# Post-norm attention layer with a LoRA-mixture FFN on one core: the last two attention parts and the FFN as one sequence, W_base in four pieces, matmuls on a constant at the start, the last tile in halves

## The chip, the core and the metric

The kernel runs on one core of a Trainium2 chip. The metric is the device time of one execution in microseconds. A core has TensorE (PE: matmuls, with its weight loads PEld beside it), VectorE (DVE), ScalarE (ACT), GpSimd (POOL) and SyncE (SP). Here SP only issues transfers. Every engine works through its own instructions in program order, and waits where an operand or a free buffer is missing.

## The reference

`x` is 2 x 512 x 512 in fp32, the attention has 32 query heads and 8 key/value heads of 128, and the FFN is a 512 x 512 linear map plus a routed low-rank part of 4 active experts of rank 8.

```python
def attn(x):                       # causal, rotary, R = 4 query heads per key head
    q, k, v = x @ Wq + bq, x @ Wk + bk, x @ Wv + bv
    p = softmax(mask(rope(q) @ rope(k).T / sqrt(128)))
    return (p @ v) @ Wo + bo

def ffn(x):
    y = x @ W_base.T + b_base
    alpha = softmax(log(prior[active] + 1e-12) + (x @ router_W.T + router_b)[active])
    return y + sum_e alpha_e * 2 * (x @ A_e.T) @ B_e.T

x = layernorm(x + attn(x))
x = layernorm(x + ffn(x))
```

## The kernel before

The order of every instruction is written out by hand (a manual schedule). The work is cut into 16 units (a key head of one batch), each unit into 4 parts (128 query tokens, times 4 heads), and each part into 4 score steps of 32 tokens times 4 heads. One `slot(T)` issues, for step T, the scores of step T, the masked maximum and the exponentials of step T-1, the reciprocals of T-2, the normalisation of T-3, the 32x32 block transposes of T-4, and so on. Four steps make a part, which `blocks_out` writes to DRAM (`db`) and `blocks_in` reads back as a fully transposed tile (`pT`). `weigh` multiplies `pT` with the values (`pc`, line 535), `context_out` copies the result (`ctxT`), and either `wo_products` (a Strassen form, for the first 14 units) or `wo_mm` with `wo_out` (plain, for the last two) adds the output projection into the residual `x_sb`. Scores stand in a PSUM pool `sc` of two buffers: the scores of step s+2 wait until the exponentials of step s have read theirs.

The stages that the change touches:

- **The start** (lines 170 to 183 and 889 to 912). POOL builds an identity, a mask row `maskw` and zeros. PE transposes the first four token tiles (`transpose_token_tile`, line 265) as they arrive, then computes the keys (line 346) and the four query heads (`q_mm`, also line 346) of unit 0, with the values (`v_tile`, line 333, added to the bias by DVE in line 338) behind query heads 1 to 3. All the value tiles use the bank `wx`. Then come the transposes of token tiles 4 to 7, and then the slots.
- **The experts.** In the first slot `gather_experts` lets DVE compute indices (lines 225 to 245), and POOL then issues eight indirect transfers (line 248), the fourth of which is `pr_act`. Four slots later `prior_weights` uses it: DVE line 295, a logarithm on ACT (line 297), DVE lines 300 to 304, and in slot -2 one tiny matmul on PE (`pl`, line 307). DVE's index computation stands behind the values `v_3` in DVE's order, and the matmul `pl` stands in PE's order behind 7 query products of unit 1.
- **W_base.** At slot `T_PROJ` = 237 the projection memory is given up and `wb_sb` is loaded into it with one transfer of 1 MB (line 924), before slot 237 issues its `blocks_in`. Its four transposes (bank `k`, copied to `wbT` by ACT, line 266) stand in slots 242 to 245. In slot 246 ACT computes two square roots for the first normalisation, which needs another activation table: the load stands before them, and another before the next exponential.
- **The end.** `Ffn` objects `f0[0]`, `f0[1]` (two tiles each of batch 0), `fa` (two tiles of batch 1), `fb` and `fc` (one tile each) go through: statistics, root, `centre`, `transpose` (x1T), `route` (`zl`), `logits`, `alphas`, `base` (four matmuls `py`, line 710), `low_rank` (`tz`, `zT`), `finish` (line 714, with the residual added by DVE in line 717), second statistics, root, `store`. The slots run to E+12 = 268, and after them the rest is written as a list. The last tile `fc` gets its residual through PE (`residual`, line 722), its statistics from PSUM (`finish_in_bank`), one scaling of 128x512 and one output transfer.

Of the kernel before, what the change touches and what calls it, by code (L numbers as in the profile page):

```python
# [9 lines left out]
F32 = mybir.dt.float32  # L10
# [5 lines left out]
P = 128  # L16
H = 32
G = 8
R = H // G
# [10 lines left out]
def postln_layer_kernel(  # L30
# [69 lines left out]
    outf = out.flatten_outer_dims()  # L100
# [13 lines left out]
    x_sb = const.tile([P, NT, HID], F32, name="x_sb")  # L114
# [16 lines left out]
    xT = proj.tile([P, KC, B * S], F32, name="xT")  # L131
# [33 lines left out]
    def load_x(t, n):  # L165
        nc.sync.dma_start(
            out=x_sb[:, t : t + n, :], in_=xf[t * P : (t + n) * P, :].rearrange("(t p) n -> p t n", p=P))


    make_identity(nc, ident)  # L170
    nc.gpsimd.memset(maskw, 0.0)

    tri = setup.tile([P, QB, BLK], F32, name="tri")
    nc.gpsimd.memset(tri, 0.0)
# [1 line left out]
        out=tri, in_=tri, pattern=[[-BLK, QB], [-1, BLK]], compare_op=ALU.is_ge,  # L176
# [84 lines left out]
    def transpose_token_tile(dst, src, pool, tag, copy):  # L261

        tp = pool.tile([P, KC, P], F32, tag=tag, name="tp")
        for c in range(KC):
            nc.tensor.transpose(tp[:, c, :], src[:, ts(c, P)], ident)  # L265
        copy(dst, tp)  # L266
# [49 lines left out]
    sc = {}  # L316
# [19 lines left out]
    def v_out(gg, t):  # L336
        v_sb[gg, t] = work.tile([P, VN], F32, tag="v", name=f"v_{gg}_{t}", bufs=11)
        nc.vector.tensor_tensor(v_sb[gg, t], psq["v", gg, t], wvs[gg][1], ALU.add)  # L338
# [191 lines left out]
    def weigh(p, j):  # L530
        u, i = parts[p]
        g, b = unit(u)
        if j == 0:
            psc[p] = ps_ctx.tile([P, R, P], F32, tag="ctx", name="pc")
        nc.tensor.matmul(  # L535
            psc[p], lhsT=v_sb[g // VG, b * TPB + j][:, ts(g % VG, D)], rhs=pT[p][:, :, ts(j, P)],
            start=(j == 0), stop=(j == i))

    def context_out(p):
        ctxT[p] = work.tile([P, R, P], F32, tag="ctxT", name=f"ctxT_{p}", bufs=3)  # L540
        nc.scalar.copy(ctxT[p], psc[p])  # L541
# [59 lines left out]
    def wo_mm(p, r):  # L601

        u, i = parts[p]
        if r == 0:
            pwo[p] = ps_wo.tile([P, HID], F32, tag=("wx", "wy")[p % 2], name="po")
        nc.tensor.matmul(  # L606
            pwo[p], lhsT=ctxT[p][:, r, :], rhs=wos[set_of(u)][:, r, :], start=(r == 0), stop=(r == R - 1))

    def wo_out(p):
        u, i = parts[p]  # L610
        t = unit(u)[1] * TPB + i
        nc.vector.tensor_tensor(x_sb[:, t, :], pwo[p], x_sb[:, t, :], ALU.add)


    class Norm:
# [4 lines left out]
            self.rstd = pool.tile([P, n], F32, name=f"rstd_{name}")  # L620
            self.pool = pool

        def stats(self, i, src):
            st = self.pool.tile([P, 6], F32, tag="st", name="st", bufs=2)
            nc.vector.bn_stats(st, src)
            nc.vector.bn_aggr(self.mv[:, i, :], st)

        def root(self, lo, hi):
# [7 lines left out]
    class Ffn:  # L636
# [15 lines left out]
            self.norm1.apply(i, self.tiles[i])  # L652

        def transpose(self, i, pool, tag):
            self.xT[i] = self.pool.tile([P, KC, P], F32, tag=f"x1T{self.where[i] % TPB}", name=f"x1T_{self.where[i]}")
            transpose_token_tile(self.xT[i], self.tiles[i], pool, tag, nc.scalar.copy)

        def route(self, i):
# [54 lines left out]
        def finish(self, i):  # L713
            nc.tensor.matmul(self.py[i], lhsT=self.zT[:, i, :], rhs=bmT, start=False, stop=True)  # L714
            t = self.where[i]
            self.y[i] = self.pool.tile([P, O], F32, tag=f"y{t % TPB}", name=f"y_{t}")
            nc.vector.tensor_tensor(self.y[i], self.py[i], self.tiles[i], ALU.add)
            self.norm2.stats(i, self.y[i])

        def residual(self, i):  # L720

            nc.tensor.matmul(self.py[i], lhsT=ident, rhs=self.tiles[i], start=False, stop=False)

        def finish_in_bank(self, i):

            t = self.where[i]
            self.y[i] = self.pool.tile([P, O], F32, tag=f"y{t % TPB}", name=f"y_{t}")
            nc.tensor.matmul(self.py[i], lhsT=self.zT[:, i, :], rhs=bmT, start=False, stop=True)
            self.norm2.stats(i, self.py[i])

        def store(self, i, src=None):
            self.norm2.apply(i, self.y[i], src)
            nc.sync.dma_start(out=outf[ts(self.where[i], P), :], in_=self.y[i])


    NP = len(parts)
# [8 lines left out]
    def put(slot, f):  # L745
        extra.setdefault(slot, []).append(f)
# [3 lines left out]
    def v_tile(gg, t, pool, tag):  # L750
        for c in range(KC):
            v_mm(gg, t, c, pool, tag)
# [135 lines left out]

    spare = ((ps_wo, "wx"), (ps_wo, "wy"), (ps_ctx, "ctx"), (ps_sc, "sc"))
    q_banks = ((ps_q, "qx"), (ps_q, "qy"), (ps_q, "qx"), (ps_wo, "wy"))  # L890
    for t in range(TPB):
        transpose_token_tile(xT[:, :, ts(t, P)], x_sb[:, t, :], *spare[t], copies[t % 2])
    tb = ps_sc.tile([P, H + G], F32, tag="sc", name="tb")
# [7 lines left out]
    for r in range(R):  # L901
        for c in range(KC):
            q_mm(0, r, c, *q_banks[r])
        for part in range(3):
            q_rope(0, r, part)
        if r:
            v_tile(0, r - 1, ps_wo, "wx")
            v_out(0, r - 1)
    v_tile(0, R - 1, ps_wo, "wx")
    v_out(0, R - 1)  # L910
    for t in range(TPB, NT):
        transpose_token_tile(xT[:, :, ts(t, P)], x_sb[:, t, :], *spare[t % 2 + 2], nc.scalar.copy)

    T_SETUP = 20
    for T in range(T_BEGIN, T_SETUP):
# [2 lines left out]
    T_PROJ = T_END - 19  # L918
# [5 lines left out]
    nc.sync.dma_start(out=wb_sb, in_=W_base.rearrange("(c p) n -> p c n", p=P))  # L924
    wbT = ffn_pool.tile([P, KC, O], F32, name="wbT")


# [3 lines left out]
    QX, QY, SC = (ps_q, "qx"), (ps_q, "qy"), (ps_sc, "sc")  # L931
    f0 = [Ffn(f"0{n}", [2 * n, 2 * n + 1], ffn_pool, K_BANK) for n in range(2)]
# [16 lines left out]
    for n, f in enumerate(f0):  # L949
        at = A + 5 + n * 8  # L950
        for k in range(2):
            put(at, lambda f=f, k=k: f.route(k))
        put(at, f.logits)
        put(at + 1, f.alphas)
        for k in range(2):
# [3 lines left out]
        for k in range(2):  # L959
            put(at + 5, lambda f=f, k=k: f.finish(k))  # L960
        put(at + 6, lambda f=f: f.norm2.root(0, 2))
        for k in range(2):
            put(at + 6, lambda f=f, k=k: f.store(k))
    put(E + 8, lambda: fa.norm1.root(0, 2))
    for k in range(2):
        put((E + 2, E + 7)[k], lambda k=k: fa.norm1.stats(k, fa.tiles[k]))
        put(E + 8, lambda k=k: fa.centre(k))
        put(E + 10, lambda k=k: fa.transpose(k, *SC))
        put(E + 11, lambda k=k: fa.route(k))
    put(E + 11, fa.logits)  # L970
    put(E + 12, fa.alphas)
    put(E + 9, lambda: (fb.norm1.stats(0, fb.tiles[0]), fb.norm1.root(0, 1), fb.centre(0)))
    put(E + 11, lambda: fb.transpose(0, *QX))
    for T in range(T_PROJ, E + 13):
        slot(T)
    for c in range(KC):
        fa.base(0, c, *SC)
    fc.norm1.stats(0, fc.tiles[0])
    fc.norm1.root(0, 1)
    fc.centre(0)  # L980
    fb.route(0)
    fb.logits()
    fb.alphas()
    fa.low_rank()
    for c in range(KC):
        fa.base(1, c, *SC)
    fc.transpose(0, *QY)
    fb.low_rank()
    fa.finish(0)
    fa.finish(1)  # L990
    fc.route(0)
    fc.logits()
    fc.alphas()
    fa.norm2.root(0, 2)
    fa.store(0)
    fa.store(1)
    for c in range(KC):
        fb.base(0, c, *QX)
    fb.finish(0)
    fc.low_rank()  # L1000
    for c in range(KC):
        fc.base(0, c, *QY)
    fc.residual(0)
    fb.norm2.root(0, 1)
    fb.store(0)
    fc.finish_in_bank(0)
    fc.norm2.root(0, 1)
    fc.store(0, fc.py[0])


# [48 lines left out]
```

## Time and profile before

The median of three runs is 849.96 us (849.74 to 852.04). The profile is one further execution.

| what | value |
|---|---|
| runs | 849.96 us median, 849.74 to 852.04 |
| the profiled execution, its own time | 849.14 us |
| its span, first to last instruction | 847.3 us |
| granted TensorE clock, mean | 0.994 |
| HBM traffic | 71.73 MB read, 44.04 MB written, 137 GB/s over the span |
| ACT exponentials, line 494 | 256 instructions, 124.2 us busy, 485 ns mean |
| PE context products, line 535 | 320 instructions, 166.4 us busy, 603 ns mean |
| PE scores, line 479 | 512 instructions, 161.8 us busy, 398 ns mean |

An fp32 matmul appears as two instructions, an fp32 transpose as one. A row of the timeline starts with the start in us from the beginning of the span and the time the merged instructions took; in square brackets stands how long the engine had been idle before, and what released it. SPq is SP's queue of transfers. A matmul's duration contains its way through the array, so that back-to-back matmuls overlap in these rows: the distance of their starts is what each costs.

### The profile page before, as it was taken

What the parts mean: (1) busy time and instruction counts of PE and PEld (TensorE: products, weight loads), DVE (VectorE), ACT (ScalarE), POOL (GpSimd) and SP (SyncE); (2) the same over time, 40 slices, a digit from 0 to 9 for tenths busy, and PEclk for the clock granted to TensorE, in tenths of its full rate; (3) what the DMA queues carried; (4) which work ended last, traced back from release to release, by engine and by line L of the source; (5) the groups of instructions that cost most, each with busy time, mean ns of one, the idle gap of its engine ahead of it and who ended that gap; (6) DMA issues with size and microseconds to landing.
All of it is one profiled execution on the core that took longest, in us unless ns stands there. A gap on an engine that the chain in (4) does not pass through costs nothing.

```text
span 847.3 us, 10606 instructions
## 1 busy us (share of the span) xinstructions
PE 827.3 (98%) x3161; PEld 573.9 (68%) x3161; DVE 594.2 (70%) x1952; ACT 351.1 (41%) x990; POOL 277.4 (33%) x308
## 2 busy tenths in 40 slices
PE   8999999999999999999999999999999999799987
PEld 4567677777777767777777777777777776554443
DVE  4468977787767877786767877786767869654354
ACT  1225454444435343444344353434444444562331
POOL 5474334233332334133332234353433324200000
PEclk9999999999999999999999999999999999999999
DMA  9017536463654555362644455472735436564201
GB/s 297 25 44 205 158 82 193 106 179 113 156 154 102 166 160 165 88 197 64 178 133 119 156 155 162 105 220 76 194 103 149 150 105 189 170 207 112 87 26 50
DMA packets 84779, 116.47 MB, mean 137 GB/s; under 512 B 6517, under 2 KB 64477, under 8 KB 82674
## 3 DMA queue, kind: packets, MB, share of 16 engines
q1 hardware_dynamic: 84210, 115.63, 47.4%
q0 software_dynamic: 448, 0.14, 0.2%
q8 instruction: 25, 0.41, 0.2%
q14 instruction: 32, 0.26, 0.1%
q10 hardware_dynamic: 64, 0.02, 0.0%
HBM read 71.73 MB, written 44.04 MB: 137 GB/s over the span
## 4 chain that ended last, share of the span: by engine, by line
PE 93%; DVE 4%; DMA 1%; ACT 1%; issue 0%; DVEq 0%; ACTq 0%
PE pc L535 16%; PE sc L479 14%; PE qx L420 11%; PE wx L420 11%; PE pp L346 10%; PE qy L420 8%; PE wy L420 8%; PE pv L333 6%; PE po L606 3%; PE py L710 3%; PE tp L265 1%; PE zl L663 1%; DMA pT<-db 1%; PE py L714 1%; DVE t L359 0%
## 5 line engine op out<-in xcount | busy, mean ns | idle before, releaser
L494 ACT ACTIVATE p<-sc,nmax 128x288 f32<-128x288 f32 (+15 forms) x256 | 124.2, 485 | 263.9 <-DVE nmax L487 207.3
L487 DVE CUSTOM_DVE_ANT_0 sc<-sc,maskw 128x288 f32<-128x288 f32 (+15 forms) x256 | 114.1, 446 | 158.3 <-PE sc L479 155.4
L535 PE MATMUL pc<-pT,v 128*128 128x512 f32 x320 | 166.4, 603 | 4.0 <-DMA pT<-db 4.0
L479 PE MATMUL sc<-kT,qT 128*128 128x160 f32 (+15 forms) x512 | 161.8, 398 | 0.2 <-ACT p L494 0.2
L502 ACT ACTIVATE p<-p,den 128x288 f32<-128x288 f32 (+15 forms) x256 | 133.5, 521 | 1.2 <-DVE den L498 1.0
L367 POOL TENSOR_TENSOR qT<-q,t 128x512 f32<-128x512 f32 x56 | 71.1, 1269 | 189.0 <-DVE q L366 189.0
L479 PEld LDWEIGHTS sc<-kT,qT 128*128 128x128 f32 x512 | 96.9, 190 | 29.6 <-issue 15.6
L407 POOL TENSOR_TENSOR cs<-ctxT 128x256 f32<-128x256 f32 x28 | 26.8, 956 | 195.6 <-PE wy L420 109.2
L541 ACT COPY ctxT<-pc 128x512 f32<-128x512 f32 x64 | 37.4, 585 | 122.8 <-PE pc L535 122.6
L510 DVE STREAM_TRANSPOSE zt<-p 128x128 f32<-128x128 f32 (+2 forms) x192 | 81.5, 425 | 0.0
L535 PEld LDWEIGHTS pc<-pT,v 128*128 128x128 f32 x320 | 57.1, 191 | 23.8 <-issue 7.0
L346 PE MATMUL pp<-xT,wk 128*128 128x512 f32 x128 | 65.0, 593 | 0.5 <-ACT xT L266 0.5
L333 PE MATMUL pv<-wv,xT 128*128 128x256 f32 x256 | 64.1, 380 | 1.1 <-DVE v L338 1.1
L333 PEld LDWEIGHTS pv<-wv,xT 128*128 128x128 f32 x256 | 48.4, 190 | 15.2 <-issue 7.4
L420 PE MATMUL wx<-wo,ctxT 128*128 128x256 f32 x224 | 58.1, 382 | 0.3 <-DVE den L498 0.3
L420 PE MATMUL qx<-xs,wq 128*128 128x256 f32 x224 | 58.0, 381 | 0.0
L512 DVE STREAM_TRANSPOSE zt<-p 128x32 f32<-128x32 f32 (+3 forms) x256 | 57.3, 224 | 0.1
L420 PEld LDWEIGHTS qx<-xs,wq 128*128 128x128 f32 x224 | 41.4, 190 | 22.3 <-issue 16.0
L420 PEld LDWEIGHTS wx<-wo,ctxT 128*128 128x128 f32 x224 | 43.0, 192 | 14.0 <-issue 8.6
L494 ACT ACTIVATION_READ_ACCUMULATOR p<-sc,nmax 128x1 f32 x256 | 49.8, 194 | 0.0
L592 DVE TENSOR_TENSOR x_sb<-wx,x_sb 128x256 f32<-128x256 f32 x112 | 46.9, 419 | 0.0
L359 DVE SCALAR_TENSOR_TENSOR t<-q,bqkT,rope_sb 64x512 f32<-64x512 f32 x56 | 43.0, 768 | 1.3
(224 smaller groups left out, 1334.8 us busy)
## 6 DMA issues: line engine op xcount, KB each, us to landing
db<-zt SPq DMA_DIRECT2D x64, 256.0 KB, 4.3
pT<-db SPq DMA_DIRECT2D x16, 1024.0 KB, 4.8
db<-zt SPq DMA_DIRECT2D x64, 192.0 KB, 3.3
pT<-db SPq DMA_DIRECT2D x16, 768.0 KB, 4.6
wq<-in_L_attn_Wq_dram SPq DMA_DIRECT2D x20, 512.0 KB, 4.9
wo<-in_L_attn_Wo_dram SPq DMA_DIRECT2D x10, 1024.0 KB, 7.5
db<-zt SPq DMA_DIRECT2D x64, 128.0 KB, 2.4
pT<-db SPq DMA_DIRECT2D x16, 512.0 KB, 4.1
```

What stands on the lines that cost most here:

```text
L333: nc.tensor.matmul(psq["v", gg, t], lhsT=xT[:, c, ts(t, P)], rhs=wvs[gg][0][:, c, :], start=(c == 0), stop=(c == KC - 1))
L346: nc.tensor.matmul(psq[key], lhsT=wt[:, c, cols], rhs=xT[:, c, ts(b, S)], start=(c == 0), stop=(c == KC - 1))
L367: nc.gpsimd.tensor_tensor(dst, t1[:].rearrange("p (n s) -> p n s", s=BLK), t2[:].rearrange("p (n s) -> p n s", s=BLK), ALU.add)
L420: nc.tensor.matmul(ps, lhsT=wt[:, c, :], rhs=xt[:, c, :], start=start and c == 0, stop=c == CH - 1, skip_group_check=True)
L479: nc.tensor.matmul(sc[s][:, :w], lhsT=qT[u][:, i * QB + n].rearrange("p r s -> p (r s)"), rhs=kT[u][:].rearrange("p n s -> p (n s)")[:, :w ...
L487: nc.vector.tensor_tensor_reduce(sc[s][:, :w], sc[s][:, :w], maskw[:, S - w :], -SCALE, -MASKED, ALU.add, ALU.min, nmax[s])
L494: nc.scalar.activation(ptile[s][:, :w], sc[s][:, :w], AF.Exp, bias=nmax[s], scale=-1.0, accum_out=rden[s])
L502: nc.scalar.activation(ptile[s][:, :w], ptile[s][:, :w], AF.Copy, scale=rden[s])
L510: nc.vector.transpose(z[:, :, last - i : last, n, :].rearrange("p q j s -> p j q s"), ptile[s][:, : i * P])
L512: nc.vector.transpose(z[:, : n + 1, last, n, :], ptile[s][:, i * P : w])
L535: nc.tensor.matmul(psc[p], lhsT=v_sb[g // VG, b * TPB + j][:, ts(g % VG, D)], rhs=pT[p][:, :, ts(j, P)], start=(j == 0), stop=(j == i))
L592: nc.vector.tensor_tensor(into, pw[k, bank], into, ALU.add)
```

## The change

- `maskw` is zeroed by DVE, and not by POOL. After it, three matmuls of 128x256 on that constant stand in front of PE's first transposes; nothing reads what they write.
- In the opening list the transposes of token tiles 4 to 7 go behind query head 2; the values follow behind heads 1 and 3 and after the loop, and alternate between the banks `wx` and `ctx`.
- `W_base` is loaded in four transfers of 256 KB at the ends of slots 237, 238, 241 and 242, behind these slots' `blocks_in`. Its transposes move from slots 242, 243, 244, 245 to 241, 242, 245, 246.
- The slots end at E+6 = 262. What followed is one list together with the last two parts' `weigh` and `wo_mm`: the second tile of `f0[1]` gets its `base` between the last `weigh` and the transposes of `fa`; the `finish` and `store` of `f0[1]` go behind the routing of `fa` and `fb`; `fa`'s second-normalisation steps go behind those of `f0[1]`.
- The last tile is computed in two halves of 256 columns in two banks: four matmuls, the residual and the low-rank part for each. Two statistics, one aggregate, two scalings, two output transfers, on SP's and on ACT's queue.
- The buffers for x1T and y have names of their own instead of shared tags.

```diff
+    nc.vector.memset(maskw, 0.0)
     make_identity(nc, ident)
-    nc.gpsimd.memset(maskw, 0.0)
...
-        def residual(self, i):
-
-            nc.tensor.matmul(self.py[i], lhsT=ident, rhs=self.tiles[i], start=False, stop=False)
...
+        def half(self, i, n, pool, tag):
+
+            cols = ts(n, O // 2)
+            py = self.py[i, n] = pool.tile([P, O // 2], F32, tag=tag, name="ph")
+            for c in range(KC):
+                nc.tensor.matmul(py, lhsT=self.xT[i][:, c, :], rhs=wbT[:, c, cols], start=(c == 0), stop=False)
+            nc.tensor.matmul(py, lhsT=ident, rhs=self.tiles[i][:, cols], start=False, stop=False)
+            nc.tensor.matmul(py, lhsT=self.zT[:, i, :], rhs=bmT[:, cols], start=False, stop=True)
...
+        def store_halves(self, i):
             t = self.where[i]
...
+            y = self.pool.tile([P, O], F32, name=f"y_{t}")
+            for n, queue in enumerate((nc.sync, nc.scalar)):
+                cols = ts(n, O // 2)
+                self.norm2.apply(i, y[:, cols], self.py[i, n])
+                queue.dma_start(out=outf[ts(t, P), cols], in_=y[:, cols])
...
+    idle = ps_sc.tile([P, 2 * P], F32, tag="sc", name="idle")
+    for _ in range(3):
+        nc.tensor.matmul(idle, lhsT=maskw[:, :P], rhs=maskw[:, : 2 * P], start=True, stop=True)
...
-        if r:
-            v_tile(0, r - 1, ps_wo, "wx")
-            v_out(0, r - 1)
-    v_tile(0, R - 1, ps_wo, "wx")
-    v_out(0, R - 1)
-    for t in range(TPB, NT):
-        transpose_token_tile(xT[:, :, ts(t, P)], x_sb[:, t, :], *spare[t % 2 + 2], nc.scalar.copy)
+        if r == 2:
+            for t in range(TPB, NT):
+                transpose_token_tile(xT[:, :, ts(t, P)], x_sb[:, t, :], *spare[t % 2 + 2], nc.scalar.copy)
+        elif r:
+            v_tile(0, r // 2, *spare[r // 2 * 2])
+            v_out(0, r // 2)
+    for t in range(2, TPB):
+        v_tile(0, t, *spare[t % 2 * 2])
+        v_out(0, t)
...
-    nc.sync.dma_start(out=wb_sb, in_=W_base.rearrange("(c p) n -> p c n", p=P))
...
-        put(T_PROJ + 5 + c, lambda c=c: transpose_token_tile(wbT[:, :, ts(c, P)], wb_sb[:, c, :], ps_k, "k", nc.scalar.copy))
+        put(T_PROJ + (0, 1, 4, 5)[c], lambda c=c: nc.sync.dma_start(out=wb_sb[:, c, :], in_=W_base[ts(c, P), :]))
+        put(T_PROJ + (4, 5, 8, 9)[c], lambda c=c: transpose_token_tile(wbT[:, :, ts(c, P)], wb_sb[:, c, :], ps_k, "k", nc.scalar.copy))
...
+    for j in range(2):
+        weigh(NP - 1, j)
+    context_out(NP - 1)
     for c in range(KC):
+        fz.base(1, c, *QY)
+    fb.norm1.stats(0, fb.tiles[0])
+    fb.norm1.root(0, 1)
+    fb.centre(0)
+    for k in range(2):
+        fa.transpose(k, *SC)
+    for r in range(R):
+        wo_mm(NP - 1, r)
+    wo_out(NP - 1)
```

More of the change, by code (lines that the diff above doesn't have):

```diff
@@ L621, in __init__, with stats @@
             self.pool = pool
-        def stats(self, i, src):
-            st = self.pool.tile([P, 6], F32, tag="st", name="st", bufs=2)
-            nc.vector.bn_stats(st, src)
+        def stats(self, i, *srcs):
+            st = self.pool.tile([P, len(srcs), 6], F32, tag=f"st{len(srcs)}", name="st", bufs=2)
+            for k, src in enumerate(srcs):
+                nc.vector.bn_stats(st[:, k, :], src)
             nc.vector.bn_aggr(self.mv[:, i, :], st)
@@ L654, in transpose @@
         def transpose(self, i, pool, tag):
-            self.xT[i] = self.pool.tile([P, KC, P], F32, tag=f"x1T{self.where[i] % TPB}", name=f"x1T_{self.where[i]}")
+            self.xT[i] = self.pool.tile([P, KC, P], F32, name=f"x1T_{self.where[i]}")
             transpose_token_tile(self.xT[i], self.tiles[i], pool, tag, nc.scalar.copy)
@@ L715, in finish, with store @@
             t = self.where[i]
-            self.y[i] = self.pool.tile([P, O], F32, tag=f"y{t % TPB}", name=f"y_{t}")
+            self.y[i] = self.pool.tile([P, O], F32, name=f"y_{t}")
             nc.vector.tensor_tensor(self.y[i], self.py[i], self.tiles[i], ALU.add)
             self.norm2.stats(i, self.y[i])
-        def residual(self, i):
-            nc.tensor.matmul(self.py[i], lhsT=ident, rhs=self.tiles[i], start=False, stop=False)
-        def finish_in_bank(self, i):
-            t = self.where[i]
[L727 to L733, printed above, removed]
+        def half(self, i, n, pool, tag):
[5 more added lines that the diff above has]
+            nc.tensor.matmul(py, lhsT=self.zT[:, i, :], rhs=bmT[:, cols], start=False, stop=True)
+        def store(self, i):
+            self.norm2.apply(i, self.y[i])
+            nc.sync.dma_start(out=outf[ts(self.where[i], P), :], in_=self.y[i])
+        def store_halves(self, i):
+            t = self.where[i]
+            y = self.pool.tile([P, O], F32, name=f"y_{t}")
[3 more added lines that the diff above has]
+                queue.dma_start(out=outf[ts(t, P), cols], in_=y[:, cols])
     NP = len(parts)
@@ L954, in postln_layer_kernel @@
         put(at + 1, f.alphas)
-        for k in range(2):
+        for k in range(2 - n):
             for c in range(KC):
@@ L958, in postln_layer_kernel @@
         put(at + 3, f.low_rank)
[L959 to L964, printed above, removed]
-    for k in range(2):
[L966 to L974, printed above, removed]
-        slot(T)
-    for c in range(KC):
-        fa.base(0, c, *SC)
+    for k in range(2):
+        put(A + 10, lambda k=k: f0[0].finish(k))
+        put(A + 11, lambda k=k: (k or f0[0].norm2.root(0, 2), f0[0].store(k)))
+    put(E + 2, lambda: fa.norm1.stats(0, fa.tiles[0]))
+    for T in range(T_PROJ, E + 7):
+        slot(T)
+    fz = f0[1]
+    CTX = (ps_ctx, "ctx")
+    fa.norm1.stats(1, fa.tiles[1])
+    fa.norm1.root(0, 2)
+    for k in range(2):
+        fa.centre(k)
+    for r in range(R):
+        wo_mm(NP - 2, r)
+    wo_out(NP - 2)
+    for j in range(2):
+        weigh(NP - 1, j)
+    context_out(NP - 1)
+    for c in range(KC):
+        fz.base(1, c, *QY)
+    fb.norm1.stats(0, fb.tiles[0])
+    fb.norm1.root(0, 1)
+    fb.centre(0)
+    for k in range(2):
+        fa.transpose(k, *SC)
+    for r in range(R):
+        wo_mm(NP - 1, r)
+    wo_out(NP - 1)
+    for k in range(2):
+        fa.route(k)
+    fb.transpose(0, *CTX)
     fc.norm1.stats(0, fc.tiles[0])
@@ L980, in postln_layer_kernel @@
     fc.centre(0)
+    fa.logits()
+    fa.alphas()
+    for k in range(2):
+        fz.finish(k)
+    for c in range(KC):
+        fa.base(0, c, *SC)
     fb.route(0)
@@ L983, in postln_layer_kernel @@
     fb.alphas()
+    fc.transpose(0, *CTX)
     fa.low_rank()
@@ L986, in postln_layer_kernel @@
         fa.base(1, c, *SC)
-    fc.transpose(0, *QY)
     fb.low_rank()
-    fa.finish(0)
-    fa.finish(1)
     fc.route(0)
@@ L993, in postln_layer_kernel @@
     fc.alphas()
-    fa.norm2.root(0, 2)
-    fa.store(0)
-    fa.store(1)
+    for k in range(2):
+        fa.finish(k)
+    fz.norm2.root(0, 2)
+    for k in range(2):
+        fz.store(k)
     for c in range(KC):
         fb.base(0, c, *QX)
+    fc.low_rank()
+    fa.norm2.root(0, 2)
+    for k in range(2):
+        fa.store(k)
     fb.finish(0)
[L1000 to L1003, printed above, removed]
+    fc.half(0, 0, *QY)
     fb.norm2.root(0, 1)
     fb.store(0)
-    fc.finish_in_bank(0)
+    fc.half(0, 1, *CTX)
+    fc.norm2.stats(0, fc.py[0, 0], fc.py[0, 1])
     fc.norm2.root(0, 1)
-    fc.store(0, fc.py[0])
+    fc.store_halves(0)
 _INS = [
```

## The prediction

> **What bounds it.** I read the page's busy shares first, then PE's waits, then the timeline around each wait.
>
> ```profile
> PE 827.3 (98%) x3161; PEld 573.9 (68%) x3161; DVE 594.2 (70%) x1952; ACT 351.1 (41%) x990; POOL 277.4 (33%) x308
> ```
>
> PE is the bound. Of 847.3 us it is idle for 20, and between 100 and 700 us the windows show it busy throughout. So time can only come from the idle 20 us, from a low clock, and from the tail. PE's own waits say where:
>
> ```profile
> PE pc L535 <- DMA pT<-db: 4.0, 1, 4.0
> PE tp L265 <- DMA x_sb<-_attn_hidden_states_dram: 3.7, 1, 3.7
> PE tp L265 <- DVE x_sb L633: 1.9, 1, 1.9
> PE pp L346 <- ACT xT L266: 1.2, 2, 0.7
> PE pv L333 <- DVE v L338: 1.1, 1, 1.1
> PE po L606 <- ACT ctxT L541: 1.0, 1, 1.0
> ```
>
> Each is aimed at by one part of the change; the other 5.6 us are the tail. The order of the changed program's instructions shows slots 0 to 236 unchanged on all engines and queues, so the stretch from 43 to 723 us should only shift.
>
> **The constant at the start.** Before, the first 16 transposes run at 0.22 us each (3.52 us), later ones at 0.11 (8 in 0.87): the clock is low until about 7. Three matmuls of two passes at 0.43 us (256 columns at the low rate) fill 1.3 to 3.9, so PE is awake before tile 3 arrives at 6.2, where PE's weight loads wait for the transfer. Tile 3's four transposes then take 0.43 and not 0.88; its ACT copy ends near 7.44 and the keys start near 7.5, against 7.86: **-0.36**. Bounds: 0 and -0.5, since tile 3's arrival stays. DVE's memset is over before PE needs it (POOL's took 0.53).
>
> Here a rule speaks against the change: the Trainium skill (TensorE: Matmul & The Clock Gate, Part 4) says transposes do not count as activity for the clock. Then 2.6 us of matmuls would be too little for the 3.4 us that Part 1 asks, and this term would be 0. The row says otherwise: after 3.5 us of transposes alone, the keys' passes start 0.43 apart from 7.86 on, the full rate. I take the row.
>
> **The opening list.** From query head 2's end at 23.43: first eight transposes to the start of the second group 1.27 (33.37 to 34.64 before, with the copy's wait in it), eight more 0.86: 25.56. Head 3, eight passes of 0.43: 29.00. Values 1, 2, 3 at 1.72 each: 34.16, where unit 1's queries start, against 36.46. The two banks remove the 1.06 wait, and head 3 hides the copies of tiles 6 and 7: **PE is 2.30 earlier**. But DVE's last value add follows its matmuls by 2.03 (31.54 to 33.57), so it moves from 33.57 to 32.44 + 2.03 = 34.47, **0.90 later**, and behind it stand the expert indices and POOL's gathers:
>
> ```profile
> 35.44 0.94 POOL L248 DMA_INDIRECT a_act<-in_L_ffn_lora_A_dram,idx_a  x1 [2.94 <-DVE idx_b L245]
> ...
> 36.46 6.28 PE L346 MATMUL pp<-xT,wq 128*128 128x512 f32 x14 [0.73 <-ACT xT L266]
> ...
> 39.11 0.88 POOL L248 DMA_INDIRECT pr_act<-_L_ffn_domain_prior_dram,full_e  x1 [0.31 <-issue]
> ...
> 41.12 0.14 DVE L295 TENSOR_SCALAR pr_eps<-pr_act 4x1 f32<-4x1 f32 x1
> ...
> 42.71 0.38 PE L307 MATMUL pl<-ident,lp_rep 4*128 4x4 f32 x2
> ```
>
> This chain is just in time before: 41.12 is 0.09 after DVE's previous instruction, and `pl` starts as the seven query products end. Now PE is ready for `pl` at 34.16 + 6.02 = 40.2, DVE sits in L295 waiting for `pr_act`, and behind L295 stand the very L362, L300 and L304 that `pl` needs. How much slack had `pr_act`? The transfer cannot have landed before its issue ended at 39.99 (slack 1.1) nor after 41.12 (slack 0). The nearest row, `a_act`, moved its bytes 1.5 to 2.1 us after its issue began, which puts `pr_act` near 41; I take slack 0.15. So `pl` comes at 42.71 + 0.90 - 0.15 - 0.36 = 43.10: the 2.30 are all waited away, and start and list together give **+0.39** (bounds -0.56 and +0.54).
>
> **The clock after that wait.** PE now idles about 3.0 us (40.1 to 43.1). The rows:
>
> ```profile
> 731.08 2.08 PE L535 MATMUL pc<-pT,v 128*128 128x512 f32 x2 [3.95 <-DMA pT<-db]
> ...
> 810.75 1.11 PE L265 MATMUL tp<-ident,x_sb 128*128 128x128 f32 x8 [1.90 <-DVE x_sb L633]
> ...
> 812.83 3.48 PE L606 MATMUL po<-wo,ctxT 128*128 128x512 f32 x4 [0.96 <-ACT ctxT L541]
> ```
>
> After 3.95 us idle `pc` takes 2.08 and not 1.02, and the next group 1.52 and not 1.03: 1.55 lost. After 1.90 the rate is still full, but the following gap of 0.96 tips it: the 4.1 us from 808.7 to 812.8 held 0.87 of transposes, and four passes took 3.31 where 1.72 is usual: 1.59 lost. The skill's Part 1 (same page) lets the clock fall after an idle window of some 3.4 us that runs freely. By the rule 3.0 us are too short: 0. By the row, a window need not be empty, a fifth of transposes did not save it, and most of a window falls into 3.0 us. I take the row: **+1.6**; the ends are 0 and 1.7.
>
> **W_base.** 1 MB waits for the last reader of the projection memory and stands ahead of `blocks_in` (57):
>
> ```profile
> 723.65 0.40 SPq L924 DMA_DIRECT2D wb_sb<-in_L_ffn_W_base_dram  x1
> 724.22 0.52 SPq L528 DMA_DIRECT2D pT<-db  x1
> ...
> 746.04 1.28 ACT L629 ACT_TABLE_LOAD   x1
> ...
> 750.14 0.66 ACT L494 ACTIVATE p<-sc,nmax 128x480 f32<-128x480 f32 x1
> ```
>
> Other parts of this size read back 3.8 us after their writes began: 717.5 + 3.8 + 4.1 landing = 725.4, in time for PE at 726.97. So `pc` comes 4.1 us earlier at full rate. Then PE is held by ACT, in four places, from the durations of these rows (score step w columns: 0.54 to 0.86; ACT exponential 0.60 to 0.72, normalisation 0.44 to 0.66, copy 0.49):
> - the second transpose waits for ACT's copy of the first, only a score product lies between: 731.11 to 731.38, 0.27;
> - the copy put ACT back, so the 320-column exponential ends at 732.94 and the 384 scores wait 0.33 (the same place waits before, at 738.01);
> - part 58's `pT` is read behind 0.5 MB of the first two pieces: write 726.1, read back 4.9 later as in other such parts, landing 4.4: 735.4 to 735.6 against 735.27, 0.3 (bounds 0 and 1.0);
> - the fourth copy now waits in ACT's order for transposes of slot 246 and stands ahead of the table load. From the 480-column scores at 740.23: product 0.86, transpose, copy end +2.8, load +4.1, roots, `ctxT`, normalisation +5.6, load +6.9, exponential end +7.6 = 747.85. The 32-column scores need it; PE is there at 746.63: 1.28. Before, that exponential ended at 750.9 and PE came at 751.78.
>
> The 32-column scores start at 747.9 against 751.78: **-3.87** (bounds -5.5, if ACT keeps up, and -2.5). SP's writes of part 58 at 726.1 stand behind the first pieces, free to go at 723.65, so they don't wait.
>
> **The end.** From 796.06, PE's last work is ready 45.47 us later. In it idle 2.05 and 1.21 (808.70 to 810.75, 811.62 to 812.83) and 1.59 of low clock, 4.85 together. In the new order `fz.base` (3.44) and the last output product cover the first chain: `fa` is centred by 801.9, its transposes come at 806.7. I followed the in-order engines to the last tile: the tightest covers are ACT's copy for `fc` (822.3 against 823.8, since one `alphas` stands ahead of it) and DVE's `zT` of `fc` (831.7 against 833.2). Gone: 4.85; added: a further switch to 33-row weights, 0.2. **-4.65** (bounds -3.2 and -4.9; each us that DVE is late costs one).
>
> **The tail.**
>
> ```profile
> 841.73 0.70 DVE L625 BATCH_NORM_STATS2 st<-py 128x6 f32<-128x512 f32 x1 [2.29 <-PE py L728]
> ...
> 843.21 0.81 DVE L633 TENSOR_SCALAR y<-py,mv_f1c,rstd_f1c 128x512 f32<-128x512 f32 x1
> ```
>
> Half of the statistics lies under PE's second half: -0.3; two scalings of some 0.43 for one of 0.81: +0.05; the last transfer has half the bytes (128 KB writes land in 2.4, 256 KB in 4.4 elsewhere, an output in 2.1): -0.25. **-0.5** (0 to -0.7).
>
> **Sum.** 849.14 + 0.39 + 1.6 - 3.87 - 4.65 - 0.5 = 842.1 on the profiled execution's scale. Its time lies 0.6 below the lowest run shown and 0.8 below the median; I add 0.6: **842.7**.
>
> **Rivals.**
> - *The clock holds through the 3 us* (the rule): 841.1. For: 1.90 idle did not do it. Against: the gap with transposes in it did.
> - *The gathers don't bind*, `pr_act` lands a full us before its reader or L295 is passed early: the opening list keeps its 2.30, no clock loss: 849.14 - 2.66 - 3.87 - 4.65 - 0.5 = 837.5, with 0.6: 838.1. Against: indices stand behind `v_3` on DVE.
> - *ACT and `pT` give more back*: W_base gains 1.5, the end 3.2: 842.7 + 2.4 + 1.4 = 846.5. For: ACT's place in slots 241 to 248 is tight.
> - *Slower*: the shifted start lets each later unit's `pT` come late against PE. 16 units of 47.3 us follow, some 15 affected; from 0.5 us each it outweighs the 7 won, at 1.1 us each the time is 859. Against: orders and queues are unchanged there and PE never waits between 100 and 700.
> - *It doesn't act*: the pieces still delay `pT`, the end waits anew: 849.5.
>
> **Numbers.** Forecast 0.40, clock holds 0.27, gathers free 0.12, gives back 0.14, slower 0.04, no effect 0.03. Range 838.0 to 846.5: it takes in the first four but for their outer bounds. A measurement tells 0.3%, 2.5 us, from no change: faster 0.93, same 0.03, slower 0.04.
>
> **What shows it.** PE idle near 3 us before `pl` and passes at twice their distance behind it (right), or `pp` running into `pl` (wrong); `pc` of part 57 without a wait; a wait for ACT before the 32-column scores; no PE gap over 0.5 us after 796 less the shift; a copy wait at the fourth W_base transposes. The forecast fails by most if PE doesn't wait at `pl`, or if `pT` 58 is later than 1 us.

## The result, and the profile after

The changed kernel takes 844.56 us in the median of six runs (843.36 to 847.94); the kernel before, measured beside it, 851.41 us. The ratio is 0.9929, 95% interval 0.9907 to 0.9951, that is 6.0 us (4.2 to 7.9): faster by more than the 0.3% that a measurement can tell. 842.7 was predicted, with a range of 838.0 to 846.5. The total is right, but some of its steps are not.

The profiled execution took 845.97 us (span 844.2 us), 3.2 us less than the profiled one of before. The page's line of busy time and the first four rows of PE's waits (us in total, times, longest):

```profile
PE 830.7 (98%) x3179; PEld 578.1 (68%) x3179; DVE 595.3 (71%) x1955; ACT 348.2 (41%) x988; POOL 276.6 (33%) x307
```

```profile
PE pl L307 <- DVE lp_rep L304: 3.2, 1, 3.2
PE idle L902 <- DVE maskw L170: 1.5, 1, 1.5
PE sc L479 <- ACT p L494: 1.2, 1, 1.2
PE pp L346 <- ACT xT L266: 0.5, 1, 0.5
```

The 4.0 us for part 57's `pT` and both waits at the end are gone. In their place stand the 3.2 us at `pl` and the 1.2 us for ACT's exponential that the prediction names. PE's busy time rose by 3.4 us, 2.9 of them the matmuls on the constant.

**The start.** Timeline of the changed kernel, PE's rows:

```profile
1.48 2.93 PE L902 MATMUL idle<-maskw 128*128 128x256 f32 x6 [1.48 <-DVE maskw L170]
4.20 1.91 PE L265 MATMUL tp<-ident,x_sb 128*128 128x128 f32 x8
6.44 1.67 PE L265 MATMUL tp<-ident,x_sb 128*128 128x128 f32 x8 [0.32 <-DMA x_sb<-_attn_hidden_states_dram]
8.03 0.25 PE L906 MATMUL tb<-ident,bqk 40*128 40x40 f32 x1
8.78 3.70 PE L346 MATMUL pp<-xT,wk 128*128 128x512 f32 x8 [0.49 <-ACT xT L266]
```

The constant holds PE until 4.2, where before the transposes began at 3.67, and here it hardly sped them up: the second eight take 1.67 us, where the first eight, at the low rate, take 1.91. The keys start at 8.78 against 7.86, 0.92 *later*.

**The opening list and `pl`.** The same timeline, all engines:

```profile
40.90 0.88 POOL L248 DMA_INDIRECT pr_act<-_L_ffn_domain_prior_dram,full_e  x1 [0.30 <-issue]
...
42.91 0.14 DVE L295 TENSOR_SCALAR pr_eps<-pr_act 4x1 f32<-4x1 f32 x1 [3.29 <-DMA pr_act<-_L_ffn_domain_prior_dram,full_e]
...
44.49 0.38 PE L307 MATMUL pl<-ident,lp_rep 4*128 4x4 f32 x2 [3.16 <-DVE lp_rep L304]
...
44.80 1.72 PE L346 MATMUL pp<-xT,wq 128*128 128x512 f32 x2
...
46.32 3.03 PE L333 MATMUL pv<-wv,xT 128*128 128x256 f32 x8
```

DVE sat 3.29 us in front of `pr_act`, PE 3.16 in front of `pl`. Behind it two query passes take 1.72 (1.13 before) and eight value passes 3.03 (1.89 before).

**W_base.** The product of part 57 runs straight behind the 288-column scores of slot 240, and PE waits for ACT's exponential in front of the 32-column scores, which began at 751.78 before:

```profile
730.13 0.65 PE L479 MATMUL sc<-kT,qT 128*128 128x288 f32 x2
730.61 1.02 PE L535 MATMUL pc<-pT,v 128*128 128x512 f32 x2
...
751.77 0.41 PE L479 MATMUL sc<-kT,qT 128*128 128x32 f32 x2 [1.24 <-ACT p L494]
```

**The end.** PE's rows in front of tile `fb`'s dense products, and these:

```profile
823.75 0.98 PE L665 MATMUL zl<-arT,x1T 128*128 128x36 f32 x8
824.66 1.98 PE L716 MATMUL py<-bmT,zT_1a 33*128 33x512 f32 x4
826.58 5.40 PE L712 MATMUL py<-wbT,x1T 128*128 128x512 f32 x8
```

Granted clock in the column behind the engines' busy times, for stretches of the last 20 us (the columns: stretch, its length, busy time of PE, PEld, DVE, ACT and POOL, the clock, the transfers' share and GB/s):

```profile
826.00:827.00 1.00, 1.00 (x3) 0.30 (x2) 0.93 (x4) 0.99 (x2) 0.00 (x0) 0.93 0.00 0
827.00:828.00 1.00, 1.00 (x2) 0.33 (x1) 0.93 (x3) 0.17 (x1) 0.00 (x0) 0.50 0.00 0
828.00:829.00 1.00, 1.00 (x2) 0.33 (x1) 0.96 (x3) 0.00 (x0) 0.00 (x0) 0.50 0.00 0
829.00:830.00 1.00, 1.00 (x3) 0.41 (x2) 0.93 (x4) 0.29 (x1) 0.00 (x0) 0.50 0.00 0
830.00:831.00 1.00, 1.00 (x4) 0.49 (x3) 0.71 (x2) 0.00 (x0) 0.00 (x0) 0.87 0.00 0
```

PE is busy all the time, and yet the clock is at half. The shares 0.93 and 0.87 put the fall at 826.86 and the return at 830.26: 3.4 us. Tile `fb`'s four dense products take 5.40 us in it and not 3.60.

From these rows the 3.1 us between the two spans add up:

| stretch | before | after | difference |
|---|---|---|---|
| span's start to `pl` | 42.71 | 44.49 | +1.78 (start 0.92, list 0.86) |
| `pl` to the 288-column scores of slot 240 | 683.77 | 685.64 | +1.87 (low clock: 1.7 of it in the first 4.7) |
| those scores to `pc` at 791.77 / 791.87 | 65.29 | 61.74 | -3.55 (W_base) |
| from there to the end of the span | 55.53 | 52.33 | -3.20 (end and tail, with 1.8 of low clock) |

### The profile page after: what moved, and what is told of

Same layout as the page of the kernel before. It is cut to its first block, busy times and chain, and to the rows that moved or that the text cites. A ratio compares the mean times of both kernels' runs of the same rounds, so it can differ in the third digit from the quotient of the medians.

```text
span 844.2 us, 10656 instructions
## 1 busy us (share of the span) xinstructions
PE 830.7 (98%) x3179; PEld 578.1 (68%) x3179; DVE 595.3 (71%) x1955; ACT 348.2 (41%) x988; POOL 276.6 (33%) x307
## 4 chain that ended last, share of the span: by engine, by line
PE 92%; DVE 4%; DMA 1%; POOL 1%; ACT 1%; issue 1%; SPq 0%; DVEq 0%; POOLq 0%
PE pc L535 16%; PE sc L479 13%; PE qx L420 11%; PE wx L420 11%; PE pp L346 9%; PE qy L420 8%; PE wy L420 8%; PE pv L333 7%; PE py L712 3%; PE po L606 3%; PE tp L265 1%; PE py L716 1%; PE zl L665 1%; DMA x_sb<-_attn_hidden_states_dram 1%; PE ph L727 0%
```

## The experiments

Ratios are to the kernel before, measured beside each, with 95% intervals. The clock turned out to differ from run to run, so a single profile shows a mechanism and only the runs show its mean. Kernels that were not measured beside each other are compared through their ratios; where medians are compared, the ratio's figure stands beside them.

### One part of the change at a time

Four kernels, each the one before with one part.

`constant_only`:

```diff
-    nc.gpsimd.memset(maskw, 0.0)
+    nc.vector.memset(maskw, 0.0)
...
+    idle = ps_sc.tile([P, 2 * P], F32, tag="sc", name="idle")
+    for _ in range(3):
+        nc.tensor.matmul(idle, lhsT=maskw[:, :P], rhs=maskw[:, : 2 * P], start=True, stop=True)
```

> The kernel before with the three matmuls on the constant and VectorE's memset, nothing else. Theory A (insurance: the clock is decided in windows of 3.41 us whose place against the kernel changes from run to run; with work from 1.5 us on, a full window always ends before the keys, without it some runs start the keys at half rate): the keys always run at full rate; median 1 to 2 us below the kernel before. Rival B (the prediction's account: tile 3's transposes at full rate, nothing else): 0.36 us below. Rival C (what the changed kernel's profile shows, the first transposes 0.53 later): 0.5 to 0.9 us above.

850.09 us against 851.09: ratio 0.9982 (0.9970 to 0.9995), by the ratio 1.5 us faster. In its profile the keys start at 8.56, later than the 7.86 of before: the profile alone would have said slower. By the size of the gain this is theory A, and the keys of this one profile ran at full rate; the interval (0.4 to 2.6 us) only just leaves rival B's 0.36 out.

`list_only` (the list as in the diff of the change):

> The kernel before with the opening list of the changed one alone. Theory A (PE comes 2.3 us earlier to the unit's queries, the gathers 0.9 later, PE waits about 3 us before pl, and the clock falls behind it): 0.9 + 1.8 = 2.7 us slower than the kernel before. Rival B (the loss between 35 and 50 us in the changed kernel came from the shifted start): 2.3 us faster.

854.05 us, ratio 1.0033 (1.0020 to 1.0047), 2.8 us *slower*. PE's waits show the price:

```profile
PE pl L307 <- DVE lp_rep L304: 3.2, 1, 3.2
```

With the start undisturbed (keys at 7.80), `pl` comes at 43.52 against 42.71, and the two groups behind it take 1.88 and 2.88. Theory A: the list alone brings PE to its queries some 2.3 us earlier, and this becomes 3.2 us of waiting with 1.7 us of half clock behind it.

`wbase_only` (four transfers and the moved transposes, as in the diff of the change):

> The kernel before with W_base in pieces alone. Theory A (the part acts by itself): part 57's product without its wait and without the low clock behind it, ACT's wait at the 32-column scores 1.2 us, in all 3.5 us faster. Rival B (it only works with the end's new order, or gives its gain back there): less than 1.5 us faster.

848.17 us, ratio 0.9967 (0.9950 to 0.9984): 2.8 us faster, the expected 3.5 lies in the interval (1.4 to 4.3). The wait for ACT before the 32-column scores is there with 1.2 us. In this execution `pc` still waited 1.2 us for a `pT`, and the wait at the end of the old sequence was followed by some 10 us of low clock in a row (0.53 mean from 810 to 815, 0.50 from 815 to 820). The part acts by itself.

`end_only` (the sequence behind E+6 and the halves):

> The kernel before with the end as one sequence and the last tile in halves alone. Theory A (both waits and the low clock behind them are gone; the new order strings thin matmuls together, 36 columns and 33 rows, and in about half of the runs one window of low clock, 1.7 us, falls on such a string): 5.0 us faster less 0.9, so 4.1 us in the median, with runs some 1.7 us apart. Rival B (no low clock of its own): 5.0 to 5.2 us faster.

848.91 us, ratio 0.9965 (0.9949 to 0.9980): 3.0 us faster (1.7 to 4.3), so the expected 4.1 is within it and 5.0 is not. Runs reach from 845.0 to 849.98. In its profile the end itself holds: from the twelve output products at 801.17 to the end of the span it takes 46.3 us, with the clock at full rate.

Together the four parts make 4.5 us by their ratios, and the whole change 6.0; the intervals are wide enough for both to be true.

### The gathers

```diff
-    put(T_BEGIN, gather_experts)
...
         if r == 2:
+            gather_experts()
             for t in range(TPB, NT):
```

`early_gathers` is the changed kernel with this edit.

> The changed kernel with the expert gathers called behind query head 2 instead of behind the last value of the opening list. Theory A (the gathers set when pl starts, and PE's 3.2 us without work set the low clock behind it): pr_act is issued near 32.6 and landed before its reader stands at the head of VectorE's order; pl starts with the end of the seven query products, near 41.4 instead of 44.49; the eight value matmuls behind it take 1.9 and not 3.0; the kernel is 3.2 + 1.8 = 5.0 us faster than the changed one, near 839.6. Rival B (something else is late next at pl, such as VectorE's rotations or the table load): pl gains under 1 us. Rival C (the low clock is a matter of chance and not of the wait): pl gains 3.2 but the clock still falls near 45; 3.2 us faster.

839.42 us in the median, ratio 0.9876 (0.9853 to 0.9899). The timeline around `pl`:

```profile
32.12 0.88 POOL L248 DMA_INDIRECT pr_act<-_L_ffn_domain_prior_dram,full_e  x1 [0.30 <-issue]
...
38.94 0.14 DVE L295 TENSOR_SCALAR pr_eps<-pr_act 4x1 f32<-4x1 f32 x1
...
40.55 0.38 PE L307 MATMUL pl<-ident,lp_rep 4*128 4x4 f32 x2
```

`pr_act` is issued 8.8 us earlier than in the changed kernel, DVE reaches line 295 without waiting, `pl` runs straight behind the seven query products (34.45 + 6.1), and the groups behind take 1.12 and 1.89. The medians differ by 5.1 us (4.5 by the ratios), where 3.2 + 1.8 = 5.0 was expected. Rival C (clock by chance) would have given 3.2, which the runs alone do not exclude. The profiles do: in all four with the wait of 3.2 to 3.3 us at `pl` (the changed kernel, `list_only`, `no_constant`, `long_constant`) the clock falls there, and in none of the nine without it. So theory A: both the wait and the clock come from the gathers' place.

### The constant, taken away and made longer

`no_constant` is the changed kernel with this edit; `both` is the same with the gathers early.

```diff
-    idle = ps_sc.tile([P, 2 * P], F32, tag="sc", name="idle")
-    for _ in range(3):
-        nc.tensor.matmul(idle, lhsT=maskw[:, :P], rhs=maskw[:, : 2 * P], start=True, stop=True)
```

> The changed kernel without the three matmuls on the constant; the memset stays on VectorE. Theory A (the constant only delays the transposes, from 3.67 to 4.20, and wakes nothing): transposes from about 3.7, keys near 7.9 instead of 8.78, and the whole kernel 0.5 to 0.9 us faster than the changed one. Rival B (the late arrival of the hidden states' third tile in that one profile was the cause, and the constant is harmless or of use): keys no earlier than 8.3, kernel 0 to 0.4 us slower or the same.

> The changed kernel without the constant and with the gathers called behind query head 2. If the two effects are separate, they add: 5.5 to 5.9 us faster than the changed one, near 839. If PE's later start was hidden behind the gathers' chain alone (so that the constant costs nothing once the chain is gone, or the other way round), no faster than early_gathers.

Both went against the expectation that I had read out of the one profile. `no_constant`: 846.36 us, ratio 0.9948 (0.9929 to 0.9968), 1.8 above the changed kernel (1.6 by the ratios). `both`: 841.31 us, 0.9894 (0.9875 to 0.9914), 1.9 above `early_gathers` (1.5 by the ratios). Each interval alone overlaps its partner's; with `constant_only` that makes three pairs, all in favour of the constant, by 1.0 to 1.9 us of median. The start of `no_constant` shows what it can prevent:

```profile
3.78 1.94 PE L265 MATMUL tp<-ident,x_sb 128*128 128x128 f32 x8 [3.78 <-DMA x_sb<-_attn_hidden_states_dram]
6.24 1.97 PE L265 MATMUL tp<-ident,x_sb 128*128 128x128 f32 x8 [0.53 <-DMA x_sb<-_attn_hidden_states_dram]
8.14 0.33 PE L903 MATMUL tb<-ident,bqk 40*128 40x40 f32 x1
8.89 5.33 PE L346 MATMUL pp<-xT,wk 128*128 128x512 f32 x8 [0.42 <-ACT xT L266]
```

Here the keys take 5.33 us and not 3.70. Over all executions that have a profile (`long_constant`, with its twenty matmuls, left out) the start of the first query product, behind the keys, is:

| | keys at full rate | keys partly at half rate |
|---|---|---|
| without the constant | 11.40 (before), 11.34, 11.82, 11.41 | 14.06, 14.60, 14.90 |
| with the constant | 12.31 (the changed kernel), 11.60, 12.10, 11.89, 11.27 | none |

The means are 12.8 and 11.8. The constant delays the first transposes by some 0.5 us in each of these profiles (4.20 against 3.54 to 3.80). The first query then comes 0.3 us later in the mean than in the warm starts without it (11.83 against 11.49), and some 2.7 us earlier than in the cold ones. The pair in the two profiles (11.40 and 12.31) is nearly the most unfavourable that could be drawn.

In the three cold starts PE waited 0.53 to 0.75 us for the third tile; in the four warm ones without the constant it did not. That this gap, and not only the place of the clock's windows, matters shows in a pair. `list_only` (warm) and `end_only` (cold, gap 0.55) record the fall of the clock after part 57's wait at the same place, 733.56 by the share 0.78 (columns as above, `list_only` first):

```profile
733.00:734.00 1.00, 0.35 (x1) 0.35 (x2) 0.00 (x0) 0.00 (x0) 0.00 (x0) 0.78 1.08 401
733.00:734.00 1.00, 0.00 (x0) 0.00 (x0) 0.00 (x0) 0.00 (x0) 0.00 (x0) 0.78 1.09 398
```

If the windows run on evenly, they stood alike at the start of both. Whether the constant helps by its work or by the delay, which shortens that gap (0.32 us in the changed kernel), no run separates.

`long_constant` is the changed kernel with this edit:

```diff
-    for _ in range(3):
+    for _ in range(20):
         nc.tensor.matmul(idle, lhsT=maskw[:, :P], rhs=maskw[:, : 2 * P], start=True, stop=True)
```

> The changed kernel with twenty matmuls on the constant instead of three: at the low rate of 0.49 us a pair of passes they would end near 1.5 + 20 x 0.98 = 21. Theory A (zeros do count as work for the clock, three were only too short: 2.76 us of the window of 3.41 us before 4.24): the passes get to half their distance between 4.9 and 8.3 us after the span's start, and the transposes behind them run at 0.11 each. Rival B (a matmul on zeros does not count): the constant stays at the low rate to its end, and the transposes behind it run at 0.22.

It takes 853.96 us, in one run; what counts are the stretches. Columns as above, with the number of PE's instructions in the first bracket:

```profile
3.00:4.00 1.00, 1.00 (x4) 0.82 (x3) 0.00 (x0) 0.10 (x1) 0.82 (x5) 1.00 1.09 369
...
5.00:6.00 1.00, 1.00 (x5) 0.82 (x4) 0.00 (x0) 0.00 (x0) 1.00 (x2) 1.00 0.98 289
6.00:7.00 1.00, 1.00 (x7) 0.87 (x6) 0.00 (x0) 0.00 (x0) 1.00 (x2) 1.00 1.04 319
```

From about 5.5 the passes come at double the rate, seven and not four in a microsecond counting those that overlap an edge, and the sixteen transposes behind take 1.91 us in all. So a matmul on zeros does count as work; theory A. (The clock's column reads 1.00 until the first change is recorded: at the start only durations tell.)

### Thin matmuls at the end

`thin_strings` is the kernel `both` with the edit below; the dense products that it puts between the two strings are left out here.

```diff
     fc.route(0)
+    for _ in range(8):
+        for c in range(KC):
+            nc.tensor.matmul(
+                fc.zl[:, 0, :], lhsT=fc.xT[0][:, c, :], rhs=arT[:, c, :], start=(c == 0), stop=(c == KC - 1))
...
+    for _ in range(8):
+        nc.tensor.matmul(fb.py[0], lhsT=fb.zT[:, 0, :], rhs=bmT, start=False, stop=False)
```

> The kernel of the run named both (no constant, gathers early) with work added in the end sequence: the 36-column product of the last tile eight times more, then three dense products more whose result nobody reads, and further on eight more 33-row products added into tile fb's accumulator, so that this tile's output holds its low-rank part nine times. Theory A (matmuls of 36 columns or 33 rows leave the clock's window without enough activity, though PE is never idle): the profile shows PE busy and the clock at 0.5 from within each string; eight 36-column products are some 7.8 us and the eight 33-row ones some 6.9, longer than two windows of 3.41, so a whole window falls into each whatever the phase. If only one kind counts as thin, the clock falls in that string alone. Rival B (the low clock at the end comes from something else): the clock stays at 1.0 through both strings.

The granted clock by stretches, columns as before:

```profile
823.00:826.00 3.00, 3.00 (x29) 3.00 (x28) 0.00 (x0) 0.00 (x0) 0.00 (x0) 1.00 0.00 0
826.00:827.00 1.00, 1.00 (x8) 1.00 (x7) 0.00 (x0) 0.00 (x0) 0.00 (x0) 0.58 0.00 0
827.00:834.00 7.00, 7.00 (x35) 7.00 (x34) 0.00 (x0) 0.00 (x0) 0.00 (x0) 0.50 0.00 0
...
840.00:847.50 7.50, 7.47 (x18) 3.04 (x16) 0.00 (x0) 0.00 (x0) 0.00 (x0) 1.00 0.00 0
...
857.00:863.00 6.00, 6.00 (x8) 1.89 (x7) 0.00 (x0) 0.00 (x0) 0.00 (x0) 0.50 0.23 86
```

PE is busy without a gap. The 36-column string starts at 822.3, and the clock is at half from 826.2 on; with dense products in between it returns; the 33-row string starts at 851.2, and the clock is at half again from 856.9. Strings of both kinds were followed by half clock, so theory A: both count as too little work. The changed end has two such strings: the routing of `fa`, four transposes and two `finish` (4.2 us), and a small transpose, the routing of `fc` and two `finish` (2.9 us). Which of them meets a window differs from execution to execution: of seven with this end sequence, three had 3.4 us of low clock there (the changed kernel and `long_constant` on the second string, `both` on the first) and took 47.8 us from the twelve output products to the end of the span; four had none and took 46.1 to 46.3. (The old order has one such string of 3.5 us, from 827.93 on, and no low clock on it in its profile.)

### ScalarE's wait, and the strings broken up

`roots_c` is `early_gathers` with the roots put first in their slot; `spread` is `roots_c` with the strings mixed with dense halves.

```diff
+    put(A + 1, lambda: [f.norm1.root(0, 2) for f in f0])
     for c in range(OC):
...
-    put(A + 1, lambda: [f.norm1.root(0, 2) for f in f0])
```

> The run named early_gathers (constant kept, gathers early) with the FFN's square roots put ahead of the fourth W_base transposes in their slot. Theory A (the 1.2 us for which PE waits at the 32-column scores come from ScalarE's order, where the table load for the roots stands behind a copy that waits 2.1 us for PE): the load moves into that idle time, the wait for ScalarE before the 32-column scores goes or falls under 0.3, 0.9 to 1.2 us faster than early_gathers, near 838.3. Rival B (something else is late next, such as the statistics that the roots need): under 0.4 us.

837.62 us, ratio **0.9839 (0.9814 to 0.9863)**, 1.8 us of median below `early_gathers` (3.2 by the ratios), more than the wait is worth; the two intervals overlap slightly, so the reading rests on the profile. ACT's timeline in `early_gathers`:

```profile
741.06 0.59 ACT L266 COPY wbT<-tp 128x512 f32<-128x512 f32 x1 [2.10 <-PE tp L265]
741.65 1.28 ACT L631 ACT_TABLE_LOAD   x1
742.95 0.48 ACT L631 ACTIVATE rstd_a<-mv_a,eps_sb 128x2 f32<-128x2 f32 x2
```

and in `roots_c`:

```profile
739.04 1.28 ACT L631 ACT_TABLE_LOAD   x1
740.34 0.48 ACT L631 ACTIVATE rstd_a<-mv_a,eps_sb 128x2 f32<-128x2 f32 x2
741.13 0.59 ACT L266 COPY wbT<-tp 128x512 f32<-128x512 f32 x1 [0.31 <-PE tp L265]
```

The load and the roots fill the idle time in front of the copy, and no wait for ACT before scores is left (1.2 us in `early_gathers`). Theory A. This version is faster than both kernels.

```diff
+    fa.base(0, 0, *SC)
+    fa.base(0, 1, *SC)
     fb.transpose(0, *CTX)
...
-    for k in range(2):
-        fz.finish(k)
-    for c in range(KC):
-        fa.base(0, c, *SC)
+    fz.finish(0)
+    fa.base(0, 2, *SC)
+    fa.base(0, 3, *SC)
+    fz.finish(1)
...
+    fb.base(0, 0, *QX)
+    fb.base(0, 1, *QX)
+    fa.finish(1)
```

> As roots_c, and the end sequence's thin matmuls (36 columns, 33 rows, transposes) mixed with the halves of the dense W_base products, so that at least half of every stretch of 3.4 us is dense. Theory A (thin strings set off the low clock at the end in some runs): no low clock after 790 in the profile, and the runs lie closer together; 0.5 to 1.2 us below roots_c in the median. Rival B (the order costs more in waits for the vector and scalar engines than the clock gives): the same or slower than roots_c.

838.39 us, ratio 0.9848 (0.9826 to 0.9869). No low clock after 790 while PE works, and five runs within 1.6 us where `roots_c` spreads over 2.9 (four of its five within 0.8, though); but the median is 0.8 higher. From the twelve output products to the end it takes 47.1 us against 46.1. PE has no gap in that stretch either; with each further change between dense and thin weights a group takes some 0.1 longer (1.96 for two base products where 1.88 is usual, 1.08 for a routing where 0.98 is). By the medians rival B, but the intervals overlap.

## Why the prediction was right, step by step

- **The constant, -0.36: the step failed.** It let the constant wake PE before tile 3 and speed that tile's transposes. In the profile it delayed the first transposes by 0.53 and sped up next to nothing. Tile 3 did run at full rate in two of the five profiles with three matmuls, where the sixteen transposes took 3.19 (`early_gathers`) and 2.86 (`spread`) and not 3.5 to 3.7. Even so the keys came at 8.06 and 7.74, against 7.86 before. The rows of `spread`:

```profile
4.20 2.86 PE L265 MATMUL tp<-ident,x_sb 128*128 128x128 f32 x16
...
7.74 3.70 PE L346 MATMUL pp<-xT,wk 128*128 128x512 f32 x8 [0.49 <-ACT xT L266]
```

  What the constant is worth shows only over several executions: with it the keys met the full rate in all five, without it in four of seven. Its mean effect is larger than predicted, 1.0 to 1.9 us of median in three pairs (1.5 to 1.6 by the ratios).
- **Row against rule, at the start.** The prediction took the row (16 transposes woke the clock) against the Trainium skill (TensorE: Matmul & The Clock Gate, Part 4), by which transposes don't count. The runs side with the row: in the kernel before, `list_only`, `wbase_only` and `both` nothing but transposes ran before keys at full rate. But it was one draw of several: in three other executions without the constant, where the third tile came 0.5 to 0.75 us late, the same transposes were followed by keys at half rate.
- **The opening list: PE 2.30 earlier, the gathers 0.90 later: right.** With the start's shift taken out, the queries came 2.22 earlier and the last value add 0.87 later. **"I take slack 0.15": wrong, it was 0.** `pr_act` takes 2.01 us from its issue to its reader in both kernels.
- **The clock after the 3 us, +1.6: right.** 1.7 measured from `pl` to the next queries (4.69 against 2.99), and gone in `early_gathers`. The rival that the clock holds fell. The rule that was weighed here (Part 1 of the same page: an idle window of some 3.4 us that runs freely) is not at odds with it, if a window need only lie *mostly* in the wait: the one that ended at 45.2 held 0.7 us of work.
- **The rival with free gathers** was priced at 838.1; the experiment that frees them gave 839.4.
- **W_base, -3.87: right,** 3.66 at the 32-column scores in the profile (3.55 by 791), 2.8 (1.4 to 4.3) alone. The 1.28 us of ACT in it measured 1.2, and its cause, the copy ahead of the table load, is shown by `roots_c`.
- **The end and the tail, -4.65 and -0.5: right where the clock holds.** In the four executions without low clock there, the 46.1 to 46.3 us are 4.7 to 4.9 less than before (51.0 from the same place of the order), for 5.15 predicted. In the profiled one it is 3.20, because the step "gone: 4.85; added: 0.2" left out what thin matmuls do to the clock. It looked for gaps in PE and found none, rightly; a gap is not what it takes.
- **"I add 0.6": too little.** The profiled execution of before, 849.14, is below all 35 runs of it that one comparison had (849.2 to 853.58, median 851.09). It had drawn warm keys and one window per wait. With 2.0 for 0.6 the sum would have been 844.1.

The mechanisms of `pl`, of the clock behind it, of W_base and of the covered waits were right. That the total came within 2 us is in part luck: between the two profiles the gain was 3.2 and not 7.0, and what the constant and the thin strings took from it came back because the profile of before was a fast draw, and that of the changed kernel, at 845.97, the second slowest of six. What remains open is how much of the run-to-run spread is the clock's; its windows were only seen in one execution per kernel.

## What to carry to other kernels

Work that is moved ahead of an in-order engine's wait gains nothing until the chain that ends the wait starts earlier too: a reorder of the opening list cost 2.8 us alone, and with eight gathers moved by a few lines `pl` came 2.2 us earlier than in the kernel before (40.55 against 42.71). Look at a PE that is never idle for strings of narrow or shallow matmuls, since the clock can fall there; but mixing them with dense ones has a price of its own. And where a cost depends on where the clock's windows fall and on when data arrive, take the mean of runs: a pair of profiles had the sign of the constant's effect wrong.

## What the hardware showed that was not expected

- The low clock comes in whole windows: 826.86 to 830.26 and, from the shares 0.60 and 0.69 around `pl`, 45.2 to 48.6 in the changed kernel, both 3.4 us, and three times that in a row in `wbase_only`. That agrees with the window of some 3.4 us that the Trainium skill names (TensorE: Matmul & The Clock Gate, Part 1). The two waits of the old end, nearly the same in four profiles, were followed by no low clock in `constant_only`, by one window in the kernel before and in `list_only`, and by three in `wbase_only`.
- A PE busy to 100% with products of 36 columns or 33 rows falls to half clock, here 3.9 and 5.7 us after the string began.
- Matmuls on zeros wake the clock like others: by about 5.5 us in `long_constant`, with work from 1.5 on.
